# A graph attention layer over sorted edges: 64 instead of 16 groups of edges computed without gathering, in four rounds

## The chip, the cores and the metric

The kernel runs on one core of one Trainium2 chip. The metric is the device time of one execution in microseconds, as the median of several runs.

## The reference

One layer of a graph network with attention, a residual sum and a layer norm. N = 12,500 nodes with 64 features, E = 400,000 edges with 64 features. Edges come sorted by destination; destinations are drawn as 12500 times the square of a uniform number, so the first nodes have by far the most edges.

```python
h_src, h_dst = x[src], x[dst]
e = leaky_relu(concat([h_src, h_dst, edge]) @ W_attn + b_attn, 0.01)[:, 0]
m = concat([h_src, edge]) @ W_ne
alpha = segment_softmax(e, dst)                    # over the edges of one destination
z = segment_sum(alpha[:, None] * m, dst)
out = layernorm(x + relu(concat([x, z]) @ W_out))  # eps 1e-5, no scale
```

## The kernel before

**Groups and batches.** A group is 512 edges (`GE`), 128 partitions by 4 (`T`); there are 782 groups. 16 of them (`BS`) make a batch; the last three batches hold 12, 12 and 6 (`ENDS`). A batch is cut into tiles of four groups (`SG`). The first `DG` groups, "dense" groups, are in no batch; here `DG` is 16, which leaves 766 groups in 49 batches.

**Gathers.** For every group of a batch, POOL issues four indirect DMAs (`gather`, L271). Each fetches 128 rows of sources into a `zx` tile; a row is a score part (one number) and x (64 numbers), from `table` in DRAM, which the front writes. In batch 0 the rows come from x itself. There are eight `zx` tiles, two batches' worth. Nothing else runs on POOL during the loop.

**A batch.** `scores` (per tile, as its rows arrive) forms the raw scores of its edges and a one-hot matrix `hot` of the edges' destinations among a window of `S` nodes. `softmax` (once a batch, behind the last tile's scores) runs scans over the 2048 edges and yields `alpha`. It calls `fill()` at four pauses. `weights` multiplies `hot` by `alpha`, `products` sums rows of `zx` by matmul into a PSUM bank `pg`, and `add_in` adds the bank into `acc`, a ring of sums by node. The products of the first two tiles (`NOW`) follow the batch's own softmax; those of the other two go on the list `later` and are done in the pauses of the next batch's softmax (`some_products`). A tile's buffer is free for POOL when its products are done.

**Finished nodes.** When all edges of a block of four times 128 nodes are in `acc`, `finish0` to `finish3` compute the output of these nodes, in pieces spread over the batches. `due` says behind which batch a block may go.

**Dense groups.** The first 16 groups belong to a handful of nodes each, so their rows need not be gathered. Three steps replace it, spread over the batches two groups at a time (`EACH`):

- Picks (batches 1 to 8). `look_turn` and `look_products` form on ACT and PE a one-hot matrix of the sources' low seven bits times the score parts of all nodes; `look_scores` picks on DVE by the high bits and adds the edge part and the destination part.
- A dense softmax behind batch 8 (`softmax` with `d`), its weights put into `kept`.
- Counts (batches 9 to 16). `dense_counts` and `dense_sum` build, for all 12,500 sources, the sum of weights by destination (`counts`); `dense_weights` and `products` with k = None add the edge features into `acc`. `resolve` multiplies `counts` by x (L418), picks the diagonal blocks on DVE (L421, L424) and adds the result into `acc`.

**Order.** The order on PE, DVE, ACT and SP in the loop is the order in which the program is written (`manual_schedule`): each engine runs its instructions in that order and waits for whatever the next one needs. POOL runs ahead through the gathers as lists of sources arrive and zx tiles come free. In the last two tiles of a batch (slots 0 and 1 of `EACH`), and in the softmax pauses (`meanwhile`), the dense work is placed:

```python
slot = i - (len(lots[k]) - EACH)
...
def meanwhile():
    while seen:
        look_scores(*seen.pop(0))
    if open_counts:
        dense_sum(*open_counts.pop(0))
    add_up(1)
    some_products()
```

**The front.** Before the loop, the score parts of all nodes are computed, `table` is written, destination windows are gathered, and the dense groups' lists are loaded and split (`dense_list`, `dense_places`), while POOL gathers batch 0 from x.

**A fallback.** The kernel looks at the data's spread while it runs (`fars`, `ups`, `lates`, `earlies`, `raised`) and runs a general path behind this one if a bound does not hold.

Of the kernel before, what the change touches and what calls it, by code (L numbers as in the profile page):

```python
# [9 lines left out]
F32 = mybir.dt.float32  # L10
# [5 lines left out]
P = 128  # L16
T = 4
# [17 lines left out]
DB = 1  # L35
EACH = 2
NOD = 5
# [10 lines left out]
def sorted_path(ctx, tc, x, dst, idx, edge, w_ne, w_attn, b_attn, w_out, out, flag):  # L48
# [43 lines left out]
    SD_ = width(DG)  # L92
    NK = len(sizes)

    def node_at(e, sigmas):
        e = e + sigmas * (e * (1.0 - e / E)) ** 0.5
        return int(N * (max(e, 0.0) / E) ** 2)

    bases = [node_at(g * GE, -5.0) for g in range(DG)]
    assert all(node_at((g + 1) * GE, 5.0) < b + NOD for g, b in enumerate(bases))  # L100
    ND = max(bases[d * BS + BS - 1] + NOD - bases[d * BS] for d in range(DB))
    HC = min(8, P // ND)

# [3 lines left out]
    mrows = [const.tile([1, 2, P + 2], F32, name=f"tops{i}") for i in range(2)]  # L107
    srows = [const.tile([1, 2, P + 2], F32, name=f"dens{i}") for i in range(2)]
    for i in range(2):
        nc.vector.memset(d3s[i], N)  # L110
        nc.vector.memset(mrows[i], FLOOR)
        nc.vector.memset(srows[i], 0.0)
# [19 lines left out]
    fars = const.tile([P, NK + 2 * DB], F32, name="fars")  # L132
    ups = const.tile([P, NK + DB], F32, name="ups")
    earlies = const.tile([P, NK + DB + 1], F32, name="earlies")
# [11 lines left out]
    low, high, place, kept, slot_, y_dense = (  # L146
        const.tile([P, T, DG], F32, name=n) for n in ("low", "high", "place", "kept", "slot_", "y_dense"))
    d3d = [const.tile([P, P + 2], I32, name=f"dense_edges{d}") for d in range(DB)]
    for d in range(DB):
        nc.vector.memset(d3d[d], N)  # L150
    counts = const.tile([P, NB, ND], F32, name="counts")
    own = const.tile([HC * ND, HC], F32, name="own")
    nc.vector.tensor_reduce(own, ident[0:HC * ND, 0:HC * ND].rearrange("p (h n) -> p h n", n=ND), axis=AX.X, op=OP.add)
    node = const.tile([HC * ND, ND], F32, name="node")
    nc.vector.tensor_reduce(node, ident[0:HC * ND, 0:HC * ND].rearrange("p (h n) -> p n h", n=ND), axis=AX.X, op=OP.add)
    meet = const.tile([1, 2], I32, name="meet")
    of_next = const.tile([1, 4], F32, name="of_next")
    held = const.tile([1, 2], F32, name="held")
# [24 lines left out]
    soft = psum.tile([P, 512], F32, name="soft", bufs=1)  # L183
    yraw, ev, scan1, scan2 = cut(soft, T * BG, P, P, P)
# [11 lines left out]
    def dense_list(d):  # L196

        srcs = pre.tile([P, BS, 2 * T], I32, name="dense_srcs", bufs=1)
        nc.sync.dma_start(out=srcs, in_=idx[d * BS:(d + 1) * BS].rearrange("g p c -> p g c"))
        return srcs  # L200

    def dense_places(d, srcs):
# [10 lines left out]
        for c, by in ((NK + d, d0b[:, at]), (NK + DB + d, base_row[:, at])):  # L213
            to = slot_ if c == NK + d else place
            nc.vector.tensor_tensor(to[:, :, at], pp, by.unsqueeze(1).to_broadcast([P, T, BS]), op=OP.subtract)
            nc.vector.tensor_reduce(fars[:, c:c + 1], to[:, :, at], axis=AX.XY, op=OP.max)
            nc.vector.tensor_scalar(fars[:, c:c + 1], fars[:, c:c + 1], 1.0 - (SD_ if c == NK + d else NOD), None, op0=OP.add)
        nc.vector.tensor_reduce(earlies[:, NK + d:NK + d + 1], place[:, :, at], axis=AX.XY, op=OP.min)
        nc.vector.scalar_tensor_tensor(place[:, :, at], high[:, :, at], -float(NOD), place[:, :, at], op0=OP.mult, op1=OP.subtract)

# [142 lines left out]
    def look_scores(g, j, loads, found):  # L363
# [16 lines left out]
        nc.vector.tensor_reduce(y_dense[:, :, g], total.rearrange("p c t -> p t c"), axis=AX.X, op=OP.add)  # L380

    def dense_counts(g):
# [3 lines left out]
        for t in range(T):  # L386
# [3 lines left out]
            nc.vector.tensor_scalar(lows[:, t, :], count_, low[:, t, g:g + 1], kept[:, t, g:g + 1],  # L390
# [7 lines left out]
    def dense_sum(g, to):  # L398

        b = bases[g] - bases[g // BS * BS]  # L400
        at = counts[:, :, b:b + NOD]
        nc.vector.tensor_tensor(at, at, to.rearrange("p (h n) -> p h n", n=NOD), op=OP.add)

    def dense_weights(g0, n):

        w = work.tile([P, SG, T, S], F32, name="w", bufs=4)[:, :, :, 0:SD_]
        for j in range(n):
            nc.vector.tensor_tensor(w[:, j], slots[:, 0:SD_].unsqueeze(1).to_broadcast([P, T, SD_]),
                                    slot_[:, :, g0 + j:g0 + j + 1].to_broadcast([P, T, SD_]), op=OP.is_equal)
            nc.vector.tensor_tensor(w[:, j], w[:, j], kept[:, :, g0 + j:g0 + j + 1].to_broadcast([P, T, SD_]), op=OP.mult)  # L410
        return w

    def resolve(d):
# [6 lines left out]
        mine = big().rearrange("l p t -> l (p t)")[0:HC * ND, 0:HC * D].rearrange("p (h f) -> p h f", f=D)  # L420
        nc.vector.tensor_tensor(mine, pairs[0:HC * ND, 0:HC * D].rearrange("p (h f) -> p h f", f=D),  # L421
                                own.unsqueeze(2).to_broadcast([HC * ND, HC, D]), op=OP.mult)
        sums_ = work.tile([P, D], F32, name="sums_", bufs=1)
        nc.vector.tensor_reduce(sums_[0:HC * ND, :], mine.rearrange("p h f -> p f h"), axis=AX.X, op=OP.add)  # L424
        if d + 1 < DB:
            nc.vector.memset(counts, 0.0)
        z = psum.tile([P, SG, P], F32, name="pg", bufs=4)[0:D, 0, 0:ND]
        nc.tensor.matmul(z, sums_[0:HC * ND, :], node, start=True, stop=True)
        at = acc[0:D, bases[d * BS]:bases[d * BS] + ND]
        nc.vector.tensor_tensor(at, at, z, op=OP.add)  # L430
# [10 lines left out]
    def turned(table_):  # L441
        line = tiny.tile([1, 2, P], F32, name="line")
# [1086 lines left out]
```

## Time and profile before

| | |
|---|---|
| median of 3 runs | 3908.24 us (3907.86 to 3909.37) |
| profiled execution, its own time | 3900.66 us |
| span of the profiled execution | 3898.9 us |
| busy: POOL | 2900.7 us (74%), 3080 instructions |
| busy: DVE | 1753.5 us (45%), 4329 instructions |
| busy: PE matmul, weight load | 1685.3 us (43%), 1541.1 us (40%) |
| busy: ACT | 729.7 us (19%) |
| mean granted TensorE clock | 0.617 |

The span runs from the first to the last instruction on the core. Busy shares are of the span. PE's matmuls and weight loads overlap. A group in the profile is one source line with one kind of instruction: its count, its busy time and mean duration, then the idle time of the engine just in front of it and what ended that idle time ("issue": nothing the profile shows).

### The profile page before, as it was taken

What the parts mean: (1) busy time and instruction counts of PE and PEld (TensorE: products, weight loads), DVE (VectorE), ACT (ScalarE), POOL (GpSimd) and SP (SyncE); (2) the same over time, 40 slices, a digit from 0 to 9 for tenths busy, and PEclk for the clock granted to TensorE, in tenths of its full rate; (3) what the DMA queues carried; (4) which work ended last, traced back from release to release, by engine and by line L of the source; (5) the groups of instructions that cost most, each with busy time, mean ns of one, the idle gap of its engine ahead of it and who ended that gap; (6) DMA issues with size and microseconds to landing.
All of it is one profiled execution on the core that took longest, in us unless ns stands there. A gap on an engine that the chain in (4) does not pass through costs nothing.

```text
span 3898.9 us, 30077 instructions
## 1 busy us (share of the span) xinstructions
PE 1685.3 (43%) x7735; PEld 1541.1 (40%) x7735; DVE 1753.5 (45%) x4329; ACT 729.7 (19%) x1711; POOL 2900.7 (74%) x3080
## 2 busy tenths in 40 slices
PE   0254334354555445533444334533354334543364
PEld 0244334343344334433344324432344334433363
DVE  5443334443444434443444434544444444544465
ACT  1111111132222211121111111111111111111121
POOL 6777777777777777777777777777777777777773
PEclk9999999975555555555555555555555555555555
DMA  9323223232333223232323223322323223223221
GB/s 119 71 62 68 56 57 71 55 66 54 62 61 66 55 51 64 54 65 54 64 54 65 54 53 66 64 50 60 61 60 67 55 54 67 61 53 63 53 59 30
DMA packets 456065, 236.40 MB, mean 61 GB/s; under 512 B 298371, under 2 KB 406906, under 8 KB 455882
## 3 DMA queue, kind: packets, MB, share of 16 engines
q0 software_dynamic: 98272, 102.21, 16.7%
q1 hardware_dynamic: 354566, 131.85, 14.1%
q8 instruction: 63, 1.03, 0.1%
q14 instruction: 120, 0.98, 0.1%
q10 hardware_dynamic: 3044, 0.33, 0.1%
HBM read 227.47 MB, written 6.68 MB: 60 GB/s over the span
## 4 chain that ended last, share of the span: by engine, by line
POOL 43%; issue 18%; PE 18%; DVE 10%; DMA 9%; ACT 1%; DVEq 1%; SPq 0%; POOLq 0%; ACTq 0%
POOL zx L271 43%; PE pg L634 13%; DMA zx<-table,srcs 7%; DVE acc L651 1%; DMA zx<-in_x_dram,srcs 1%; PE pg L841 1%; PE lines L436 1%; DVE hot L314 1%; DVE pr L319 1%; DVE sdst L322 1%; PE lines L439 1%; PE pg L840 1%; DVE level L575 1%; PE pg L395 1%; DVE soft L531 0%
## 5 line engine op out<-in xcount | busy, mean ns | idle before, releaser
L271 POOL DMA_INDIRECT zx<-table,srcs x3000 | 2830.3, 943 | 914.3 <-issue 869.5
L634 PEld LDWEIGHTS pg<-w,zx 128*128 128x128 f32 x5984 | 1286.0, 329 | 62.7 <-issue 31.6
L634 PE MATMUL pg<-w,zx 128*128 128x12 f32 (+10 forms) x5984 | 1292.5, 387 | 41.9 <-issue 24.6
L436 PE MATMUL lines<-ident,bnd 128*1 128x128 f32 x200 | 57.4, 388 | 1676.4 <-ACT bnd L534 1663.5
L436 PEld LDWEIGHTS lines<-ident,bnd 128*1 128x1 f32 x200 | 12.8, 95 | 1689.4 <-ACT bnd L534 1670.9
L312 DVE TENSOR_TENSOR fixed<-fixed,zx 128x16 f32<-128x16 f32 (+2 forms) x196 | 36.2, 184 | 1353.7 <-DMA zx<-table,srcs 1351.3
L305 DVE TENSOR_TENSOR pr<-ze,fixed 128x1024 f32<-128x1024 f32 (+2 forms) x196 | 234.3, 1195 | 113.9 <-ACT fixed L302 113.6
L302 ACT ACTIVATE fixed<-wrow 128x144 f32<-128x144 f32 (+9 forms) x196 | 50.2, 256 | 1022.2 <-DVE soft L323 444.7
L307 DVE TENSOR_REDUCE fixed<-pr 128x16 f32<-128x1024 f32 (+2 forms) x196 | 235.9, 1203 | 6.7
L395 PE MATMUL pg<-big,lows 128*128 128x490 f32 x128 | 90.9, 878 | 279.0 <-DVE lows L390 271.7
L303 ACT ACTIVATE zx<-ze 128x1024 f32<-128x1024 f32 (+2 forms) x196 | 203.8, 1040 | 10.6 <-DMA zx<-table,srcs 1.3
L651 DVE TENSOR_TENSOR acc<-acc,pg 128x12 f32 (+11 forms) x782 | 141.7, 181 | 93.9 <-DVE acc L651 27.6
L529 ACT ACTIVATE soft<-turned 128x128 f32<-128x128 f32 x50 | 19.5, 389 | 865.0 <-DVE turned L527 850.9
L395 PEld LDWEIGHTS pg<-big,lows 128*128 128x128 f32 x128 | 36.8, 303 | 327.3 <-issue 163.0
L617 DVE TENSOR_TENSOR w<-hot,fixed 128x576 f32<-128x576 bf16 (+9 forms) x196 | 103.2, 585 | 51.3 <-PE pg L634 51.3
L314 DVE TENSOR_TENSOR hot<-fixed,drel 128x576 bf16<-128x576 f32 (+9 forms) x196 | 116.9, 597 | 7.5 <-DVE fixed L312 0.8
L319 DVE TENSOR_TENSOR pr<-hot,fixed 128x576 f32<-128x576 bf16 (+9 forms) x196 | 116.1, 592 | 6.7
L322 DVE TENSOR_REDUCE sdst<-pr 128x16 f32<-128x192 f32 (+11 forms) x196 | 116.0, 592 | 6.8
L572 DVE SCALAR_TENSOR_TENSOR soft<-mask,lines,soft 128x128 f32<-128x128 f32 x50 | 18.0, 360 | 143.4 <-PE lines L439 143.4
L271 POOL DMA_INDIRECT zx<-in_x_dram,srcs x64 | 61.8, 966 | 27.2 <-issue 17.7
L481 ACT ACTIVATE same<-step 128x129 f32<-128x129 f32 x50 | 15.6, 312 | 332.4 <-DVE ups L479 332.4
L841 PE MATMUL pg<-both,acc 128*128 128x64 f32 x184 | 63.2, 447 | 19.5 <-DVE acc L651 16.3
(234 smaller groups left out, 1667.9 us busy)
## 6 DMA issues: line engine op xcount, KB each, us to landing
ze<-in_edge_dram SPq DMA_DIRECT2D x184, 512.0 KB
zx<-table,srcs POOLq DMA_INDIRECT x3000
table<-xall SPq DMA_DIRECT2D x7, 455.0 KB
out_dram<-yo SPq DMA_DIRECT2D x24, 128.0 KB
ze<-in_edge_dram SPq DMA_DIRECT2D x8, 384.0 KB
edges_of<-in_dst_dram SPq DMA_DIRECT2D x184, 8.1 KB
xall<-in_x_dram SPq DMA_DIRECT2D x13, 224.0 KB
srcs<-in_idx_dram SPq DMA_DIRECT2D x45, 64.0 KB
```

Source lines behind the costliest of these rows:

```text
L271: nc.gpsimd.indirect_dma_start(out=zx[0:r, g, t, 1:EW] if plain else zx[0:r, g, t, 0:EW], out_offset=None, in_=x[:, :] if plain else table ...
L303: nc.scalar.activation(zx[0:r, 0:n, :, EW:EW + D], ze[0:r, 0:n], AF.Copy)
L305: nc.vector.tensor_tensor(pr[0:r, 0:n], ze[0:r, 0:n], w_edge[0:r].unsqueeze(1).to_broadcast([r, n, T, D]), op=OP.mult)
L307: nc.vector.tensor_reduce(ysum[0:r, 0:n], pr[0:r, 0:n], axis=AX.X, op=OP.add)
L314: nc.vector.tensor_tensor(hot[0:r, 0:n], slots[0:r, 0:Sk].unsqueeze(1).unsqueeze(1).to_broadcast([r, n, T, Sk]), drel[0:r, :, b:b + n].rea ...
L319: nc.vector.tensor_tensor(at[0:r, 0:n], hot[0:r, 0:n], win[0:r, 0:n, 0:Sk].unsqueeze(2).to_broadcast([r, n, T, Sk]), op=OP.mult)
L322: nc.vector.tensor_reduce(sdst[0:r, 0:n], at[0:r, 0:n], axis=AX.X, op=OP.add)
L395: nc.tensor.matmul(to, lows[:, t, :], highs[t], start=(t == 0), stop=(t == T - 1))
L436: nc.tensor.transpose(in_order(line), col, ident)
L617: nc.vector.tensor_tensor(w[0:r, 0:n], hot[0:r, 0:n], alpha[0:r, :, b:b + n].rearrange("p t g -> p g t").unsqueeze(3).to_broadcast([r, n, ...
L634: nc.tensor.matmul(pg[:, g, :], zx[:, g, t, 1:EW + D], w[:, g, t, :], start=(t == 0), stop=(t == T - 1))
L651: nc.vector.tensor_tensor(ag, ag, pg[r0:P, g, :], op=OP.add)
```

## The change

`DB` goes from 1 to 4: four rounds of 16 dense groups, 64 in all, so 718 groups remain in 46 batches (three batches of 16 fewer). Each round has its picks, its dense softmax and its counts; the counts of one round run in the same batches as the picks of the next. Picks of round d fall in batches 8d + 1 to 8d + 8, the dense softmaxes behind batches 8, 16, 24 and 32, counts in 9 to 40.

- Dense sums have an array of their own, `accd`, indexed by the true node number, which is read from memory at run time (`node_of`); before, the sums with x went to places in `acc` fixed at compile time. It is added to `acc` when blocks 1 to 3 are finished; node block 0 is finished apart, after the last dense sum.
- Products with x are done after every fourth dense group (`CH`), for windows of 16 nodes (`ND`): `node_products` on PE behind the first tile's scores, `node_pick` on DVE ahead of the third tile's, `node_sum` behind the fourth's. `counts` is cleared for each.
- Edge features' sums get a place of their own in PSUM (`z_edge`), where they took a bank `pg`: `edge_products` behind the first tile's scores, `edge_sum` ahead of the third's. `dense_weights` uses a tile `wd` of its own.
- Picks and counts are issued one tile earlier (`slot = i - 1`) and taken up on DVE ahead of the next tile's scores, not in the softmax's pauses.
- Behind a batch with a dense softmax all four tiles go on `later`, and the dense softmax's pauses run `some_products`.
- Some buffers are halved (`tops`, `dens`, `line`, `rw`, `sq`), and `high` and `slot_` are bf16.

The core of the diff:

```diff
-DB = 1
+DB = 4
 EACH = 2
+CH = 4
+ND = 16
+HC = 8
...
-    SD_ = width(DG)
+    SD_ = NOD
...
+    z_edge = fixed[D:P, 512 - EACH * NOD:512].rearrange("p (g n) -> p g n", n=NOD)
+    z_node = fixed[0:D, 512 - EACH * NOD - ND:512 - EACH * NOD]
...
     def dense_sum(g, to):
-        b = bases[g] - bases[g // BS * BS]
-        at = counts[:, :, b:b + NOD]
+        _, vs = nc.values_load_multi_w_load_instructions(
+            rel[0:1, g:g + 1], engines=(EngineType.DVE,), min_val=0, max_val=ND - NOD,
+            skip_runtime_bounds_check_because=within)
+        at = counts[:, :, ds(vs[0], NOD)]
         nc.vector.tensor_tensor(at, at, to.rearrange("p (h n) -> p h n", n=NOD), op=OP.add)
...
-        w = work.tile([P, SG, T, S], F32, name="w", bufs=4)[:, :, :, 0:SD_]
+        w = tiny.tile([P, EACH, T, SD_], F32, name="wd", bufs=1)
...
+    def edge_products(g0, n, ep, w):
+        for g in range(n):
+            for t in range(T):
+                nc.tensor.matmul(z_edge[:, g, :], ep[:, g, t, :], w[:, g, t, :], start=(t == 0), stop=(t == T - 1))
+    def edge_sum(g0, n):
+        for g in range(n):
+            at = accd[D:P, ds(node_of(g0 + g), NOD)]
+            nc.vector.tensor_tensor(at, at, z_edge[:, g, :], op=OP.add)
...
+    def node_pick(g0, pairs):
+        mine = big().rearrange("l p t -> l (p t)").rearrange("p (h f) -> p h f", f=D)
+        nc.vector.tensor_tensor(mine, pairs.rearrange("p (h f) -> p h f", f=D),
+                                own.unsqueeze(2).to_broadcast([P, HC, D]), op=OP.mult)
+        sums_ = work.tile([P, D], F32, name="sums_", bufs=1)
+        nc.vector.tensor_reduce(sums_, mine.rearrange("p h f -> p f h"), axis=AX.X, op=OP.add)
+        if g0 + CH < DG:
             nc.vector.memset(counts, 0.0)
+        nc.tensor.matmul(z_node, sums_, node, start=True, stop=True)
...
         def meanwhile():
-            while seen:
-                look_scores(*seen.pop(0))
-            if open_counts:
-                dense_sum(*open_counts.pop(0))
             add_up(1)
             some_products()
...
-                    slot = i - (len(lots[k]) - EACH)
+                    slot = i - 1
...
+                    if i == 2 and edges_of:
+                        edge_sum(*edges_of[0:2])
+                    if i == 2 and opened:
+                        opened = node_pick(*opened)
+                    while seen:
+                        look_scores(*seen.pop(0))
+                    while open_counts:
+                        dense_sum(*open_counts.pop(0))
                     hot = scores(g0, n, tiles[i], drel, b0, k == 0)
+                    if i == 0:
+                        if chunk_of is not None:
+                            opened = node_products(chunk_of)
+                        if edges_of:
+                            edge_products(*edges_of)
+                    if i == 3 and opened is not None:
+                        node_sum(opened)
...
-                    ws = [weights(g0, n, hot, b0) for g0, n, zx, hot in parts]
+                    for i, (g0, n, zx, hot) in enumerate(parts):
+                        later.append([k, g0, n, zx, weights(g0, n, hot, b0), b0, fac if i == 0 else None, 0, None])
...
-                    fac_d, dense_carry = softmax(k + 1, lines_of(*after), dense_carry, lambda: None, d)
+                    fac_d, dense_carry = softmax(k + 1, lines_of(*after), dense_carry, some_products, d)
```

More of the change, by code (lines that the diff above doesn't have):

```diff
@@ L196, in dense_list @@
     def dense_list(d):
-        srcs = pre.tile([P, BS, 2 * T], I32, name="dense_srcs", bufs=1)
+        srcs = pre.tile([P, BS, 2 * T], I32, name="dense_srcs", bufs=DB)
         nc.sync.dma_start(out=srcs, in_=idx[d * BS:(d + 1) * BS].rearrange("g p c -> p g c"))
@@ L212, in dense_places @@
         nc.scalar.activation(pp, srcs[:, :, T:2 * T].rearrange("p g t -> p t g"), AF.Copy)
[L213 to L219, printed above, removed]
+        to, c = slot_[:, :, at], slice(NK + d, NK + d + 1)
+        nc.vector.tensor_tensor(to, pp, d0b[:, at].unsqueeze(1).to_broadcast([P, T, BS]), op=OP.subtract)
+        nc.vector.tensor_reduce(fars[:, c], to, axis=AX.XY, op=OP.max)
+        nc.vector.tensor_scalar(fars[:, c], fars[:, c], 1.0 - NOD, None, op0=OP.add)
+        nc.vector.scalar_tensor_tensor(place[:, :, at], high[:, :, at], -float(NOD), to, op0=OP.mult, op1=OP.subtract)
     def listed(k):
@@ L389, in dense_counts @@
             nc.scalar.activation(hi, hi, AF.Relu, scale=-1.0, bias=1.0)
-            nc.vector.tensor_scalar(lows[:, t, :], count_, low[:, t, g:g + 1], kept[:, t, g:g + 1],
+            nc.vector.tensor_scalar(lows[:, t, :], count_, low[:, t, g:g + 1], kept[:, t, g % BS:g % BS + 1],
                                     op0=OP.is_equal, op1=OP.mult)
@@ L825, in behind_front @@
     def behind_front(c0, po):
-        a0 = c0 * P % RING
         unwrap(c0)
-        for j in range(min(NBC, NB - c0)):
-            nc.tensor.matmul(po[:, j, :], acc[:, a0 + j * P:a0 + (j + 1) * P], both, start=False, stop=True,
+        for j in range(size_of(c0)):
+            nc.tensor.matmul(po[:, j, :], sums_of(c0, j), both, start=False, stop=True,
                              skip_group_check=True)
@@ L834, in finish2 @@
     def finish2(c0, xtt):
-        n = min(NBC, NB - c0)
-        a0 = c0 * P % RING
+        n = size_of(c0)
         unwrap(c0)
```

239 lines of the change are left out of this document (128 added, 111 removed).

## The prediction

> **What bounds the kernel now.** I read the page first: the span, the groups, the chain of work that ended last. One group stands out on every count.
>
> ```profile
> span 3898.9 us, 30077 instructions
> POOL 6777777777777777777777777777777777777773
> POOL 43%; issue 18%; PE 18%; DVE 10%; DMA 9%; ACT 1%; DVEq 1%; SPq 0%; POOLq 0%; ACTq 0%
> L271 POOL DMA_INDIRECT zx<-table,srcs x3000 | 2830.3, 943 | 914.3 <-issue 869.5
> L271 POOL DMA_INDIRECT zx<-in_x_dram,srcs x64 | 61.8, 966 | 27.2 <-issue 17.7
> ```
>
> POOL is level from the second slice to the last, and the idle time in front of its gathers is "issue": a fixed pause between two instructions, not a wait for anybody. The chain gives POOL only 43%, because it steps to other engines where work happened to end together; the list of POOL's waits settles whether POOL ever stood.
>
> ```profile
> POOL zx L271 <- issue: 887.2, 2911, 0.3
> POOL zx L271 <- DMA zx<-table,srcs: 20.4, 67, 0.3
> POOL zx L271 <- PE pg L634: 12.2, 40, 0.3
> POOL zx L271 <- DMA zx<-in_x_dram,srcs: 6.5, 4, 3.5
> ```
>
> No entry on the table gathers has a longest wait over 0.3 us, which is the issue pause itself with another name. So POOL never waits for a released zx tile. Only the front has real waits (6.5 us in all). POOL's timeline gives the pitch and the tail:
>
> ```profile
> 100.62 0.94 POOL L271 DMA_INDIRECT zx<-table,srcs  x1 [0.30 <-issue]
> 3844.08 0.86 POOL L271 DMA_INDIRECT zx<-table,srcs  x1 [0.30 <-issue]
> ```
>
> 3000 gathers start within 3844.08 - 100.62 = 3743.46 us: 3743.46 / 2999 = 1.2482 us each, 79.89 us for the 64 of a batch of 16 groups. Behind the last one lie 3898.9 - 3844.9 = 54 us of tail. Windows of one batch each, set on that pitch, show whether any stage departs from it:
>
> ```profile
> core 0: us, PE busy (x) PEld busy (x) DVE busy (x) ACT busy (x) POOL busy (x), PEclk, DMA share, GB/s
> 433.10:513.00 79.90, 33.82 (x157) 32.50 (x157) 33.41 (x94) 13.15 (x32) 60.39 (x65) 1.00 0.31 63
> 752.60:832.50 79.90, 42.34 (x172) 33.48 (x173) 40.72 (x117) 26.06 (x65) 60.39 (x65) 0.91 0.29 59
> 992.30:1072.20 79.90, 41.79 (x179) 34.49 (x178) 33.90 (x94) 20.59 (x44) 60.40 (x65) 0.57 0.30 61
> 1471.60:1551.40 79.80, 43.07 (x180) 33.21 (x178) 32.85 (x81) 10.57 (x28) 60.29 (x65) 0.59 0.29 57
> 1631.30:1711.20 79.90, 35.21 (x161) 33.28 (x160) 33.61 (x83) 14.77 (x35) 60.39 (x65) 0.50 0.30 59
> 3708.20:3788.10 79.90, 54.87 (x246) 51.10 (x245) 48.99 (x125) 17.88 (x45) 60.40 (x64) 0.50 0.29 58
> ```
>
> In this order: a batch with dense picks, the one behind the dense softmax, one with dense counts, the one with the dense products with x, a plain one, a crowded one near the end. POOL takes 60.4 us of busy time in each. The kernel is a string of gathers; the other engines are about half empty.
>
> **Part 1: gathers taken away.** 16 dense groups become 64. Four gathers a group: 48 x 4 = 192 gathers fewer (2808 + 64 remain of 3000 + 64), exactly three batches. 192 x 1.2482 = 239.7 us off POOL's string, if POOL stays unblocked. With them go three batches of scores, softmax and products, which were hidden.
>
> **Part 2: dense work for 48 more groups.** It rides in the batches, two groups at a time: picks in batches 1 to 32, dense softmaxes behind batches 8, 16, 24, 32, counts in 9 to 40, products with x after every fourth group. So batches 9 to 32 now carry picks and counts together. The costs:
>
> ```profile
> L371 DVE TENSOR_TENSOR hits<-pps,high 128x392 bf16<-128x392 f32 x16 | 8.9, 555 | 0.0
> L374 DVE TENSOR_REDUCE total<-pg 128x4 f32<-128x392 f32 x16 | 9.1, 566 | 0.5
> L369 DVE TENSOR_REDUCE total<-pr 128x4 f32<-128x256 f32 x16 | 6.7, 420 | 0.6
> L379 DVE TENSOR_REDUCE total<-pr 128x4 f32<-128x16 f32 x16 | 2.7, 170 | 0.5
> L402 DVE TENSOR_TENSOR counts<-counts,pg 128x490 f32<-128x490 f32 x16 | 10.6, 660 | 23.6 <-PE pg L395 23.6
> L390 DVE TENSOR_SCALAR lows<-pps,low,kept 128x128 f32<-128x128 f32 x64 | 21.7, 401 | 0.0
> L884 DVE MEMSET counts<- 128x882 f32 x1 | 0.8, 793 | 0.1
> L360 PE MATMUL pg<-s_src,big 128*128 128x98 f32 x128 | 34.6, 449 | 72.7 <-ACT big L353 72.7
> L395 PE MATMUL pg<-big,lows 128*128 128x490 f32 x128 | 90.9, 878 | 279.0 <-DVE lows L390 271.7
> 1482.50 13.22 PE L418 MATMUL pg<-xall,counts 128*72 128x512 f32 x26
> 1495.76 0.69 DVE L421 TENSOR_TENSOR big<-pg,own 72x512 f32<-72x512 f32 x1 [12.25 <-PE pg L418]
> 1496.48 1.02 DVE L424 TENSOR_REDUCE sums__7505<-big 72x64 f32<-72x512 f32 x1
> 1479.10 0.36 DVE L651 TENSOR_TENSOR acc<-acc,pg 64x4 f32 x2 [0.62 <-issue]
> ```
>
> DVE, a batch: two picks of three wide steps at 0.56, two at 0.42 and four small ones at 0.17 = 3.2 each, 6.4; two counts of 21.7/16 + 0.66 = 2.0 each, 4.0; edge sums 0.4 and four small steps for weights, 1 together; every second batch a pick of nodes, 0.69 + 1.02, and a clearing of counts, 0.79 x 1568/882 = 1.41, with its sums 3.3. Together under 15 us on the 33.6 of a plain batch: 49, which is what DVE does in the crowded window. PE: 35.2 plain + 34.6/8 = 4.3 to twice that for picks (they ran at clock 1.00, counts at 0.57) + 90.9/8 = 11.4 for counts + 13.2 for products with x + about 1 for edges = 65 to 70 of 79.9. Both stay below POOL's 79.9, so I put this work at nothing: its cover is the time in which DVE and PE wait for gathers.
>
> **What could still block POOL** is a zx tile freed late; there are eight, so batch k + 2 takes those of batch k. Tightest is the third tile of a batch, whose products are put off into the next batch's softmax:
>
> ```profile
> 914.50 3.43 PE L634 MATMUL pg<-w,zx 128*128 128x16 f32 x16
> 939.55 0.95 POOL L271 DMA_INDIRECT zx<-table,srcs  x1 [0.30 <-issue]
> ```
>
> Its last product ends at 917.9, POOL reaches the tile at 939.5: a softmax may come 21 us late before POOL stands. The batch behind a dense softmax is the place:
>
> ```profile
> 821.15 0.19 DVE L312 TENSOR_TENSOR fixed<-fixed,zx 128x16 f32<-128x16 f32 x1 [13.29 <-DMA zx<-table,srcs]
> ```
>
> There DVE had caught up and still waited 13.3 us for the fourth tile. The change puts in front of that row two picks (6.4), the second count (2.0, behind it before), edge sums (0.4) and the pick of nodes (3.3): 12.1, so 1.2 us to spare. If DVE must also wait for the whole of the products with x (13.2), it is 12 us late, still under 21. The products with x lie in PE ahead of the picks' and counts' matmuls, so those queue behind them, but PE has nothing nearer the end in that stretch. The dense softmax now has the batch's own products in its pauses instead of behind it, which frees the first tiles earlier. SP's additions (256 KB of edges again, two 128 KB rows a batch) sit in front of the next edge load; the DMA share of 0.29 to 0.31 leaves room. Bounds for Part 2: 0 to about 10 us in each of three such batches, 30 us; a gain is excluded, since POOL has no wait there to lose. I take 0, by the waits row without a single stall.
>
> **Part 3: the front.** Three more lists of 64 KB in 32-byte pieces, rows of low parts for 64 groups, and four times the list arithmetic. The nearest rows are the one list of before and POOL's wait ahead of it:
>
> ```profile
> 69.77 0.39 SPq L199 DMA_DIRECT2D dense_srcs<-in_idx_dram  x1
> 76.14 0.22 DVE L207 TENSOR_SCALAR parted<-dense_srcs 128x64 int32<-128x64 int32 x1 [25.23 <-DMA dense_srcs<-in_idx_dram]
> 63.80 0.94 POOL L271 DMA_INDIRECT zx<-in_x_dram,srcs  x1 [3.52 <-DMA zx<-in_x_dram,srcs]
> ```
>
> A list took 6 us to land, so batch 0's scores may start up to 3 x 6 = 18 us later, plus 5 of DVE. Nothing hangs on that: the first reuse of a zx tile is 64 gathers after 100.62, at 180.5, and the first batch's weights were ready at
>
> ```profile
> 127.75 0.88 DVE L617 TENSOR_TENSOR w<-hot,fixed 128x128 f32<-128x128 bf16 x4
> ```
>
> with some 50 us over. But the traffic may hold POOL's own first gathers as at 63.80. Bounds: -6.5 (the front's waits go, if the traffic falls elsewhere) to +12 (two thirds of the three lists); I take +2, near the row of 3.5.
>
> **Part 4: the tail.** The same last three batches; the new first block is finished ahead of them, and the open block's finish stays where it was. 0, bounds -3 and +3, since only the order of a few ACT instructions differs.
>
> **Sum.** The profiled execution took 3900.7 us by its own time (1.8 more than its span), the median of the three runs is 3908.24, 7.6 above. 3900.7 - 239.7 + 2 = 3663.0 profiled; with the same 7.6 us, **3670.5**. (What a measurement of this kernel can tell from no change is some 0.2%, 8 us.)
>
> **Rivals.**
>
> *POOL stands in the dense batches.* Late softmaxes behind the dense softmax or the products with x, since DVE waits in order for PE there. Against: 21 us of room and the arithmetic above. For: both waits meet in batches 17, 25 and 33, and DVE's scores grow with the windows, which eats the 13.3. At 10 us for each of three or four: 3680 to 3710. Chance 0.13.
>
> *The added DVE work slows the gathers themselves.* DVE busy goes from 33.4 to 49.0 us between the second and the last window and POOL's 64 or 65 instructions take 60.4 in both; the counts' L390 ran in the window from 992 and cost POOL nothing. If POOL were shut out for as long as the added counts and clearings run, 48 x 21.7/16 + 15 x 1.41 = 86 us: 3757. Chance 0.02. The Trainium skill (SBUF — State Buffer, "Who interferes with whom") says that some VectorE forms take a port pair shared with GpSimd for a whole instruction and starve descriptor generation, and counts tensor_scalar among them; that speaks against this change. The windows do not show it for the forms used here.
>
> *PE becomes the bound: slower than before.* If PE's in-order queue, with picks, counts, products with x and a batch's own products, took more than 79.9 us, POOL would follow PE. The gain is gone when the 32 batches with counts take 239.7/32 = 7.5 us more each, 87.4 us; at 90 us it is 32 x 10.1 = 323 us, 3992. For: the counts matmuls average 878 ns at a low clock, so my 65 to 70 rests on overlap. Against: the crowded window holds 54.9 of matmul and 51.1 of weight loads at clock 0.50 and POOL does not stretch. Chance 0.03.
>
> *It doesn't do what it says.* A dense group may span five nodes at most, or the kernel falls back on its general path. Destinations are 12500 x u^2 sorted; at edge 32768 that is node 84, and 512 edges span 2.6 nodes. No chance given.
>
> **Chances.** Forecast (3661 to 3682: the front and tail bounds) 0.82, POOL standing 0.13, ports 0.02, PE 0.03. The low end is 3670.5 less 6.5 + 2 + 1 at the front and tail, 3661; the high end takes in most of the first rival, 3700. Faster 0.96, same 0.01, slower 0.03.
>
> **What would show it.** Right: one POOL pitch of 1.248 us from start to end, no POOL wait on table gathers above 0.3 us, windows of 79.9 us with POOL at 60.4 in batches 9 to 40, DVE near 45 and PE near 65 there, a tail of 54 us. Wrong: POOL waits for PE or DMA of several us at the batches behind a dense softmax (first rival), a mean gather above 943 ns (second), windows in which PE has no idle time and POOL's share falls (third), or an added wait before 100 us (front).

## The result: 4.4% faster, and POOL stood still for 66 us

| | before | after |
|---|---|---|
| median (lowest to highest) | 3908.39 us (3907.86 to 3909.37) | 3735.15 us (3733.94 to 3736.5) |
| ratio | | 0.9557, interval 0.954 to 0.9573 |
| profiled execution, its own time | 3900.66 us | 3736.5 us |
| its span | 3898.9 us | 3734.8 us |
| mean granted clock | 0.617 | 0.68 |

The forecast was 3670.5 us (3661 to 3700). The direction was right; 65 us of the gain are missing. The page and the waits of the kernel after, beside the rows of before in the prediction (POOL's gathers are now on L273, the scores' sum with the gathered part on L314):

```profile
span 3734.8 us, 34021 instructions
POOL 6777777777777777777777766777775777777773
POOL zx L273 <- issue: 884.0, 2684, 28.6
DVE pr L307 <- ACT fixed L304: 505.6, 60, 22.4
ACT fixed L304 <- PE fixed L427: 444.1, 28, 23.9
L273 POOL DMA_INDIRECT zx<-table,srcs x2808 | 2654.2, 945 | 921.8 <-issue 866.9
```

POOL's row of tenths now has three dips behind the middle, and its longest wait is 28.6 us where it was 0.3. "issue" hides the reason: POOL's gather waits for a free zx tile, which the profile does not name. The timeline of POOL gives the first and last gather from the table and, between them, every stand of over 0.9 us (last column: the idle time ahead of the row):

```profile
102.64 0.94 POOL L273 DMA_INDIRECT zx<-table,srcs  x1 [0.30 <-issue]
1986.49 0.94 POOL L273 DMA_INDIRECT zx<-table,srcs  x1 [3.85 <-issue]
2164.22 0.95 POOL L273 DMA_INDIRECT zx<-table,srcs  x1 [18.04 <-issue]
2331.94 0.94 POOL L273 DMA_INDIRECT zx<-table,srcs  x1 [7.95 <-issue]
2495.97 0.95 POOL L273 DMA_INDIRECT zx<-table,srcs  x1 [4.30 <-issue]
2660.00 0.95 POOL L273 DMA_INDIRECT zx<-table,srcs  x1 [4.33 <-issue]
2740.63 0.95 POOL L273 DMA_INDIRECT zx<-table,srcs  x1 [0.95 <-issue]
2848.90 0.95 POOL L273 DMA_INDIRECT zx<-table,srcs  x1 [28.55 <-issue]
3677.52 0.87 POOL L273 DMA_INDIRECT zx<-table,srcs  x1 [0.30 <-issue]
```

The seven stands sum to 67.97 us, 65.9 more than seven usual pauses of 0.3. All lie behind 1980 us, the two large ones behind the dense softmaxes of batches 24 (at 2077) and 32 (at 2757). The difference of the spans closes with that:

| term | predicted | measured, from |
|---|---|---|
| 192 gathers at 1.2482 | -239.7 | -239.7 (2808 gathers from the table, were 3000) |
| front | +2 | +2.0 (first gather at 102.64, was 100.62) |
| stands of POOL | 0 | +65.9 |
| pitch elsewhere | 0 | +5.3 (3677.52 - 102.64 = 3574.9, less 2807 x 1.2482 = 3503.7 and the stands; a gather took 945 ns, was 943) |
| tail | 0 | +2.4 (3734.8 - 3678.4 = 56.4, was 54.0) |
| sum | -237.7 | -164.1 = 3734.8 - 3898.9 |

**Where the time is lost.** Windows of two pitches (159.8 us). The first fence is the kernel before, where neither picks nor counts run at that time; the second is the kernel after, where both do (columns: window, its length, busy time and instructions of PE, PEld, DVE, ACT and POOL, then clock, DMA share, GB/s):

```profile
1641.40:1801.20 159.80, 70.43 (x318) 66.58 (x318) 67.30 (x168) 29.55 (x68) 120.79 (x129) 0.50 0.30 59
```

```profile
1641.40:1801.20 159.80, 110.07 (x418) 86.97 (x419) 88.35 (x226) 48.83 (x99) 120.83 (x128) 0.57 0.32 67
```

No engine is full: PE has 50 us of idle time in two batches, DVE 71. Yet the batches fall behind in that stretch. The transpose that opens a softmax (DVE L555) stands in the timeline of the kernel after, for batches 8, 16, 17 and 23, at

```profile
746.04 0.32 DVE L555 STREAM_TRANSPOSE turned<-soft 128x128 f32<-128x128 f32 x1
1387.93 0.32 DVE L555 STREAM_TRANSPOSE turned<-soft 128x128 f32<-128x128 f32 x1
1481.60 0.31 DVE L555 STREAM_TRANSPOSE turned<-soft 128x128 f32<-128x128 f32 x1
1975.75 0.30 DVE L555 STREAM_TRANSPOSE turned<-soft 128x128 f32<-128x128 f32 x1
```

From batch 8 to 23, 15 pitches of 79.89 us would be 1198.4; it took 1229.7. Batch 23 is 31 us late against POOL, and there the stands begin. By the same sum batch 16 is 2.8 us late and batch 17, the one behind the second dense softmax, 16.5. So 14 us came in one step, which was not won back, and the other 15 over the six batches from 17 to 23. The timeline of PE, ACT and DVE between 1667 and 1687 us shows what a batch waits for:

```profile
1667.24 0.27 ACT L304 ACTIVATE fixed<-wrow 128x112 f32<-128x112 f32 x1 [4.95 <-DVE w L642]
1669.56 13.69 PE L656 MATMUL pg<-w,zx 128*128 128x24 f32 x64
1683.18 1.87 PE L427 MATMUL fixed<-wd,ep 128*64 128x5 f32 x16
1685.09 0.27 ACT L304 ACTIVATE fixed<-wrow 128x112 f32<-128x112 f32 x1 [14.19 <-PE fixed L427]
1685.38 1.22 DVE L307 TENSOR_TENSOR pr<-ze,fixed 128x1024 f32<-128x1024 f32 x1 [12.73 <-ACT fixed L304]
```

L304 copies a tile's destination windows into the PSUM bank `fixed`; L307 multiplies by them and is the first step of the tile's scores. The change put the edge sums, `z_edge`, into ten columns of the same bank. PE writes them (L427) behind the batch's own products (L656, 13.7 us) and in every second batch behind the products with x too. ACT's copy for the second tile goes to other columns of that bank, but waits until L427 is done; DVE waits for ACT, and everything of the batch waits behind DVE. That is 28 waits of ACT with 444 us in all, up to 23.9 each. DVE's own wait for ACT's copy is 505.6 us in the kernel after; in the kernel before it was

```profile
DVE pr L305 <- ACT fixed L302: 113.6, 142, 6.6
```

**Theories.** A: this wait in the shared bank makes each batch with counts a little longer than POOL's pitch, the lead runs out (the time by which a tile comes free before POOL reaches it), and POOL stands. B: the dense softmaxes, some 22 us of DVE, ACT and PE in a row, push the batches, and the wait in the bank is covered.

### The profile page after: what moved, and what is told of

It is laid out like the page before. It is cut to its first block, busy times and chain, and to the rows that moved or that the text cites. A ratio compares the mean times of both kernels' runs of the same rounds, so it can differ in the third digit from the quotient of the medians.

```text
span 3734.8 us, 34021 instructions
## 1 busy us (share of the span) xinstructions
PE 2224.6 (60%) x8923; PEld 1801.7 (48%) x8923; DVE 2013.0 (54%) x5075; ACT 1018.3 (27%) x2205; POOL 2723.6 (73%) x2888
## 5 line engine op out<-in xcount | busy, mean ns | idle before, releaser
L273 POOL DMA_INDIRECT zx<-table,srcs x2808 | 2654.2, 945 | 921.8 <-issue 866.9
L656 PE MATMUL pg<-w,zx 128*128 128x24 f32 (+10 forms) x5600 | 1222.1, 391 | 44.2 <-issue 41.7
L656 PEld LDWEIGHTS pg<-w,zx 128*128 128x128 f32 x5600 | 1217.7, 332 | 63.5 <-issue 50.2
L397 PE MATMUL pg<-big,lows 128*128 128x490 f32 x512 | 370.8, 894 | 505.5 <-DVE lows L392 425.9
L307 DVE TENSOR_TENSOR pr<-ze,fixed 128x1024 f32<-128x1024 f32 (+3 forms) x184 | 219.2, 1191 | 505.9 <-ACT fixed L304 505.6
L304 ACT ACTIVATE fixed<-wrow 128x144 f32<-128x144 f32 (+10 forms) x184 | 48.7, 264 | 1103.6 <-PE fixed L427 444.1
L309 DVE TENSOR_REDUCE fixed<-pr 128x16 f32<-128x1024 f32 (+3 forms) x184 | 221.1, 1202 | 6.3
L440 PE MATMUL pg<-xall,counts 128*128 128x512 f32 (+1 forms) x416 | 209.8, 665 | 10.6 <-DVE earlies L1049 10.6
L305 ACT ACTIVATE zx<-ze 128x1024 f32<-128x1024 f32 (+3 forms) x184 | 191.7, 1042 | 10.5 <-issue 1.3
L314 DVE TENSOR_TENSOR fixed<-fixed,zx 128x16 f32<-128x16 f32 (+3 forms) x184 | 33.9, 184 | 287.7 <-DMA zx<-table,srcs 282.5
L390 ACT ACTIVATE big<-places,place 128x490 f32<-128x490 f32 x256 | 176.0, 687 | 0.0
L673 DVE TENSOR_TENSOR acc<-acc,pg 128x16 f32 (+10 forms) x718 | 132.2, 184 | 80.2 <-DVE acc L673 38.2
L391 ACT ACTIVATE big<-big 128x490 f32<-128x490 f32 x256 | 156.7, 612 | 8.2
L557 ACT ACTIVATE soft<-turned 128x128 f32<-128x128 f32 x50 | 19.4, 388 | 445.7 <-DVE turned L555 445.7
```

What stands on the lines that cost most here:

```text
L273: nc.gpsimd.indirect_dma_start(out=zx[0:r, g, t, 1:EW] if plain else zx[0:r, g, t, 0:EW], out_offset=None, in_=x[:, :] if plain else table ...
L305: nc.scalar.activation(zx[0:r, 0:n, :, EW:EW + D], ze[0:r, 0:n], AF.Copy)
L307: nc.vector.tensor_tensor(pr[0:r, 0:n], ze[0:r, 0:n], w_edge[0:r].unsqueeze(1).to_broadcast([r, n, T, D]), op=OP.mult)
L309: nc.vector.tensor_reduce(ysum[0:r, 0:n], pr[0:r, 0:n], axis=AX.X, op=OP.add)
L390: nc.scalar.activation(hi, places, AF.Square, bias=place[:, t, g:g + 1])
L391: nc.scalar.activation(hi, hi, AF.Relu, scale=-1.0, bias=1.0)
```

## The experiments

Except where a second kind of chip is named, the runs below fell on two chips on which the kernel before took 3901.8 and 3902.0 us. "Late" always means by the sum above: against batch 8 and a pitch of 79.89 us.

**The changed kernel again**, as the control of the runs below.

> The changed kernel itself, beside the kernel before, on the chip that the next three run on. If this chip gives its usual times, both theories expect 3735 us beside 3908 (ratio 0.956) and POOL standing still for 71 us between its gathers. If it gives 4588 us for the kernel before, as in the four runs before these, both theories expect the changed kernel above 5200 us, and the next three are then compared with this run and not with 3735.

3731.93 us, ratio 0.9564 (0.9545 to 0.9583); the stands sum to 68.2 us over the usual pauses. This is the kind of chip of the prediction, and the times below compare with 3732, or with 3731 on the second of the two chips.

**Edge products at the end of the batch before.**

```diff
                     if i == 0:
                         if chunk_of is not None:
                             opened = node_products(chunk_of)
-                        if edges_of:
-                            edge_products(*edges_of)
...
                     edges_of = (batch_counts[0], len(batch_counts), rows_again,
                                 dense_weights(batch_counts[0], len(batch_counts)))
+                    edge_products(*edges_of)
```

> The edge products are issued at the end of the batch before, ahead of that batch's own products, instead of behind the next batch's. Theory A (ScalarE's copy of the second tile's windows waits in the bank `fixed` for the edge products, which lie behind 13.7 us of the batch's own products and in every second batch behind 13.2 us of products with x): no edge product is late, the copy of the windows waits under 3 us, POOL stands under 10 us in all, 3665 us (3660 to 3675). Theory B (the 22 us of each dense softmax push the batches behind POOL, and the wait in the bank is hidden): 3735 us.

3663.69 us (3662.99 to 3664.67), ratio 0.939 (0.9375 to 0.9406). The waits:

```profile
POOL zx L273 <- issue: 818.1, 2685, 0.3
DVE fixed L314 <- DMA zx<-table,srcs: 488.3, 73, 13.9
DVE pr L307 <- ACT fixed L304: 55.0, 60, 6.6
```

POOL never stands, and the same softmaxes come at

```profile
742.36 0.32 DVE L555 STREAM_TRANSPOSE turned<-soft 128x128 f32<-128x128 f32 x1
1942.16 0.30 DVE L555 STREAM_TRANSPOSE turned<-soft 128x128 f32<-128x128 f32 x1
```

1199.8 us apart: 1.4 late in place of 31. The dense softmax behind batch 16 still makes batch 17 late, by 8.0 us, but batch 18 is only 1.2 late. DVE waits for gathers again (488 us, the kernel after 282). This is what theory A forecast. The new place is not free: in front of the edge products PE now waits 75 us in all for their weights, and DVE's own weights wait 53 us for the edge products. POOL's string shows nothing of either.

**Edge products where they were, in a bank of their own.**

```diff
     def edge_products(g0, n, ep, w):
+        z_edge = psum.tile([P, SG, P], F32, name="pg", bufs=4)[D:P, 0, 0:EACH * NOD].rearrange("p (g n) -> p g n", n=NOD)
+        edge_at.append(z_edge)
...
     def edge_sum(g0, n):
+        z_edge = edge_at.pop()
```

> The edge products stay where they are in TensorE's queue, but write a bank of the ring `pg`, taken when they are issued and free when they are added, in place of the bank `fixed`. Theory A: the copy of the windows no longer waits for them, VectorE's sums of the edges wait instead, two tiles later, when they are long done; the ring of four banks is one bank shorter for a third of a batch, which may cost up to 1 us in a batch: 3665 to 3690 us. Theory B: 3735 us. Were it the edge products' length in TensorE's queue and not the bank, it would stay at 3735 too.

3662.12 us (3661.76 to 3665.46), ratio 0.9388 (0.9372 to 0.9404):

```profile
POOL zx L273 <- issue: 815.6, 2676, 0.3
DVE pr L307 <- ACT fixed L304: 55.4, 60, 7.0
100.54 0.94 POOL L273 DMA_INDIRECT zx<-table,srcs  x1 [0.30 <-issue]
3604.24 0.87 POOL L273 DMA_INDIRECT zx<-table,srcs  x1 [0.31 <-issue]
```

The matmuls, their order and their length in PE's queue are those of the changed kernel (the edge products take 47.5 us in both); only the bank differs, and all 68 us of stands are gone. So it is the bank, not PE's time. 3604.24 - 100.54 = 3503.7 us is the unbroken string of 2808 gathers to a tenth. One bank fewer for the products in part of a batch cost nothing that can be seen. This and the one above are the fastest kernels here that do all the work, within 2 us of each other.

**The order of two calls.** In place of moving the edge products out of the batch, they go ahead of the products with x only.

```diff
                     if i == 0:
+                        if edges_of:
+                            edge_products(*edges_of)
                         if chunk_of is not None:
                             opened = node_products(chunk_of)
-                        if edges_of:
-                            edge_products(*edges_of)
```

> Only the order of two calls is swapped: the edge products go into TensorE's queue ahead of the products with x (13.2 us in every second batch), and still behind the batch's own products (13.7 us). On the first kind of chip: if both lengths of queue count alike, a pair of batches becomes 13 us shorter, 151 to 153 us against the 159.8 us of its gathers, no batch falls behind, 3663 to 3670 us. If the wait behind the batch's own products is enough by itself to make the batches fall behind, part of the stands stays: 3680 to 3715 us.

3678.72 us (3677.59 to 3683.08), ratio 0.9427 (0.9411 to 0.9442). It fell between the two ranges expected. The products with x were the larger part: of the 67 us between the changed kernel (3730.85 on the same chip) and the one with the edge products moved, 52 went with this swap. The profiled execution, the slowest of the four, still has ACT wait 309.8 us for L427, 14.7 at most, and POOL stands 1.7, 1.1 and 9.7 us. The batch's own products alone do not make one batch after the other later: batch 16 is 1.7 us late, batch 17 behind the dense softmax 15.8, batch 23 12.7. What they do is keep the batches from winning the push of a softmax back.

**Without dense softmaxes**, the wait in the bank kept. The dense groups' weights are then whatever the last scores left.

```diff
-                    fac_d, dense_carry = softmax(k + 1, lines_of(*after), dense_carry, some_products, d)
+                    lines_of(*after)
+                    fac_d = None
+                    for _ in range(4):
+                        some_products()
```

> The four dense softmaxes are left out (their weights are whatever the last scores give); every product that they covered is still issued. Theory A: the batches still fall behind by 2 to 3 us each through the bank, only the push of 22 us at the end of each round is gone: 3685 to 3715 us. Theory B: 3665 us, with no stand of POOL.

3700.28 us, one run. POOL's stands in its timeline:

```profile
2306.27 0.94 POOL L273 DMA_INDIRECT zx<-table,srcs  x1 [7.87 <-issue]
2470.39 0.94 POOL L273 DMA_INDIRECT zx<-table,srcs  x1 [4.64 <-issue]
2634.38 0.94 POOL L273 DMA_INDIRECT zx<-table,srcs  x1 [4.53 <-issue]
2812.28 0.94 POOL L273 DMA_INDIRECT zx<-table,srcs  x1 [18.37 <-issue]
3293.13 0.94 POOL L273 DMA_INDIRECT zx<-table,srcs  x1 [1.48 <-issue]
```

35 us of stands are left without any dense softmax. The first three have the size of those at 2332, 2496 and 2660 us in the kernel after; its stands of 3.9 and 18.0 are gone, and 28.6 has become 18.4. Batch 16 is 0.6 us late here, batch 23 19.4: the wait in the bank alone makes batches late, from batch 16 on. Theory B falls as the cause; but 32 us did go with the softmaxes. Are they a cost by themselves?

**Both: edge products moved, and no dense softmaxes** (the two diffs together).

> The edge products issued at the end of the batch before, and the four dense softmaxes left out as well. On the first kind of chip, if the softmaxes are hidden wherever the batches have a lead, nothing is left to win: 3661 to 3666 us; if they cost something beside their push on late batches: under 3660 us.

3661.62 us, one run, against 3663.7 with the softmaxes. With the wait the four softmaxes cost 3731.9 - 3700.3 = 32 us, without it 2, which is within the spread of runs of one kernel. They only bring out what the wait has done to the lead: a batch that is on time takes a push of 22 us and wins it back, one that is already late does not.

**Three rounds in place of four** (`DB = 3`), the wait in the bank kept.

> Three rounds of dense groups in place of four, and the wait in the bank as it was. Unbroken, POOL's string would be 79.9 us longer than in the repaired kernels: 3743 us. The picks and the counts then run together over 16 batches in place of 24. On the first kind of chip, by the theory of a lead that the batches use up: POOL stands 0 to 25 us in all, 3743 to 3768 us. If every round cost its 18 us of stands by itself: about 3793 us.

3758.05 us (3755.26 to 3758.35), ratio 0.9629 (0.9613 to 0.9645), with one stand:

```profile
2151.19 0.94 POOL L273 DMA_INDIRECT zx<-table,srcs  x1 [13.11 <-issue]
```

The time is in the range expected of a lead that is used up, and far from 18 us a round: 12.8 us of stands over 16 batches with picks and counts together, 68 over 24. A steady loss it does not show: batch 18 is 9.6 us late, batch 24 12.2, and the one stand comes with batch 25, behind a dense softmax, 36.2 us late. So the fourth round took 79.9 us of gathers away, and as the change was written 27 us of it arrived.

**A second kind of chip.** Eight runs, on two other chips, show something else altogether. The kernel before takes 4588 us there (4588.28 on one, 4587.89 on the other). The first four of these runs were to decide between A and B. Expected of the edge products at the end of the batch before, of the two calls swapped, of the dense softmaxes left out, and of the edge work left out (`edge_products` and `edge_sum`, so that the dense nodes' sums lack their edge half):

> Edit: the products of the dense edge features (into z_edge, in the PSUM bank of tile fixed) go to PE at the end of the batch before, ahead of that batch's own products, not behind the first tile's scores. Theory A (shared bank): ACT's copy of the second tile's windows into fixed waits for these products, which lie in PE behind 13.7 us of the batch's products and, in every second batch, 13.2 us of products with x; DVE idles for it, batches come later and later, and POOL stands 70 us in the end. Then the wait of ACT for the edge products goes, POOL stands under 5 us, time 3665 (3660 to 3675). Theory B (the dense softmax): its 22 us push the batch behind past what the eight zx tiles can bear, whatever stands in the bank; then POOL stands about as long as now, 3735 (3720 to 3740).

> Edit: the two calls behind the first tile's scores are swapped, edge products ahead of products with x. Theory A: the second tile's copy still waits behind the batch's own products in every batch, but no longer for the 13.2 us of products with x in every second one; a pair of batches falls from 165 us to about 152 to 158, just under POOL's 159.8, so POOL stands 0 to 15 us: 3665 to 3680. Theory B: nothing changes, 3735. If DVE's wait for the products with x at its own pick of nodes is what counts, 3735 too, since that pick comes no earlier.

> Leaves out the four dense softmaxes (the batch's own weights are taken as the dense ones); all else as in the changed kernel. Theory A: batches still fall behind by 5 to 6 us a pair while picks and counts run together (12 pairs, 60 to 70 us against 21 us of room), so POOL still stands, 20 to 50 us: 3685 to 3715. Theory B: POOL stands under 5 us, 3665.

> Leaves out the products and sums of the dense edge features altogether. Theory A: the copy of the second tile's windows has nothing to wait for, POOL does not stand, 3660 to 3668. Theory B: 3730 to 3735 (only the 1.9 us of products and 0.4 us of sums a batch go).

Four more fell on the other of these chips: the two calls swapped, three rounds, edge products moved with no dense softmaxes, and no edge work again:

> Only the order of two calls is swapped: the edge products go into TensorE's queue ahead of the products with x (13.2 us in every second batch), and still behind the batch's own products (13.7 us). If both lengths of queue count alike, a pair of batches becomes 13 us shorter, 151 to 153 us against the 159.8 us of its gathers: no batch falls behind, POOL never stands, 3663 to 3670 us. If the wait behind the batch's own products is enough by itself to make the batches fall behind, part of the 71 us stays: 3680 to 3715 us.

> The changed kernel with three rounds of dense groups in place of four (48 groups not gathered, 64 gathers more), and the wait in the bank as it was. Unbroken, POOL's string would be 79.9 us longer than in the repaired kernels: about 3743 us. The picks and the counts then run together over 16 batches (8 to 24) in place of 24, and in the changed kernel the lead that the batches have over POOL lasted just until batch 24: by the theory of the bank POOL stands 0 to 25 us in all, 3743 to 3768 us. So the fourth round, as it stands, bought little more than 10 to 35 us of the 80 us of its gathers. If the lead did not matter and every round cost its 18 us, the stands would be about 50 us and the time 3793 us.

> The edge products issued at the end of the batch before, and the four dense softmaxes left out as well. With the softmaxes left out and the wait kept POOL stood 37 us (3700 us); with the wait taken away and the softmaxes kept it never stood (3664 us). If the softmaxes cost something by themselves beside their push on late batches, it shows here: under 3660 us. If they are hidden wherever the batches have a lead, nothing is left to win: 3661 to 3666 us.

> The edge products and the sums that they go into are left out altogether (128 x 4 small matmuls and 64 sums less; the dense nodes' edge half is then missing from the output). What is left besides is the dense weights. If the move of the edge products to another bank or another place already hides all of their cost, this gains nothing over it: 3661 to 3667 us. Below 3655 us they would still cost in the repaired kernels.

All eight missed by over 1300 us:

| kernel | time there | instructions | ns of span per instruction |
|---|---|---|---|
| before | 4588 us | 30077 | 153 |
| edge products at the end of the batch | 5185.23, ratio 1.1303 (1.1284 to 1.1322) | 34068 | 152 |
| order of two calls | 5254.87, ratio 1.1446 (1.1423 to 1.1469); again 5257.47 | 34021 | 154 |
| no dense softmaxes | 5299.75 | 33774 | 157 |
| no edge products and sums | 5016.79; again 5024.67 | 32786 | 153 |
| three rounds | 5105.42, ratio 1.1131 (1.1112 to 1.1149) | 32813 | 155 |
| edge products moved and no softmaxes | 5122.96 | 33821 | 151 |

(Spans are those of the profiled executions; for the kernel before the median stands in.)

Neither theory could be tested there: this kind of chip says nothing of A and B, and as the kernel with no edge work ran on this kind alone, its forecast stays open. The page of the kernel with two calls swapped, there:

```profile
span 5255.9 us, 34021 instructions
L273 POOL DMA_INDIRECT zx<-table,srcs x2808 | 2648.9, 943 | 2446.8 <-issue 2309.0
L656 PE MATMUL pg<-w,zx 128*128 128x24 f32 (+10 forms) x5600 | 1231.9, 376 | 974.0 <-issue 907.5
```

and the same rows of the changed kernel, the control above:

```profile
L273 POOL DMA_INDIRECT zx<-table,srcs x2808 | 2650.2, 944 | 923.7 <-issue 870.4
L656 PE MATMUL pg<-w,zx 128*128 128x24 f32 (+10 forms) x5600 | 1222.1, 391 | 44.3 <-issue 41.9
```

One gather and one matmul take no longer than on the first kind. What grows is the idle time ahead of single instructions for which the profile shows no wait: PE has 907.5 us of it ahead of its plain products. On POOL it comes in lumps. Between 290 and 810 us POOL stands 6.3 to 6.8 us ahead of every 32nd gather and the usual 0.3 ahead of all others, as in

```profile
298.66 0.94 POOL L273 DMA_INDIRECT zx<-table,srcs  x1 [6.33 <-issue]
344.64 0.94 POOL L273 DMA_INDIRECT zx<-table,srcs  x1 [6.35 <-issue]
```

The traces of two more kernels there (edge products at the end of the batch, no edge work) have the same lumps in that stretch; on the first kind there is none. Over these programs time there goes along with the number of instructions, not with POOL's string; whatever adds dense work adds instructions, and every variant of the change is 9 to 16% slower than before. The changed kernel itself ran on chips of the first kind alone; its last run was expected so:

> The changed kernel itself, to show which chip the next three run on. On the first kind (kernel before 3902 us) it takes 3732 us, and the next three are read against that and against the 3664 us of the kernel with the edge products at the end of the batch. On the second kind (kernel before 4588 us) all kernels so far took 151 to 157 ns for each instruction of their profile, so that this one, with 34021 instructions, should take 5150 to 5340 us whatever the wait in the bank does.

It took 3730.85 us. So on the second kind of chip the changed kernel is not measured.

## Why the prediction was wrong

- **Part 1 was right.** 192 gathers at 1.2482 us are off the string; with the wait taken away the string is 3503.7 us as worked out, and 0.939 of the prediction's median, 3908.24, is 3669.8 us against the forecast of 3670.5. The rest of the dense work does cost nothing then, as forecast.
- **Part 2 is the step that failed**: "I put this work at nothing". Its sums of busy time were not short: two batches hold 110 of PE and 88 of DVE, 55 and 44 each, where 65 to 70 and 49 were reckoned. What failed is the sentence that the products with x delay only picks and counts, "but PE has nothing nearer the end in that stretch". It had: the edge products lie behind them, and through the bank `fixed` they hold ACT's copy and the second tile's scores. The term was taken at 0, with bounds of 0 to 30, and measured 65.9.
- The change listed `z_edge = fixed[...]`, and the prediction priced the edge matmuls (1 us) and their sums (0.4), but never asked who else uses that bank. The rule was to be had: the Trainium skill (PSUM — Partial Sum Buffer, "PSUM bank collisions raise a hardware error") says that engines must be kept apart by bank and group of partitions, not by address. Here the two writers share 64 partitions of one bank and no column, and the traces show them kept apart, at 444 us of ACT's waits; a bank of its own ends it. What keeps them apart the traces do not say, and whether the columns could be written at the same time was not tried.
- **"1.2 us to spare", "21 us late before POOL stands".** The room was the right quantity and nearly of the right size (the first stand, 3.6 us, came with batch 23 31 us late, so some 28 us of room), but it was spent in one place, the batch behind a dense softmax. It is a stock: the 14 us of one softmax were still missing when the next 15 came. Without the wait the same softmax costs 8.0 us at batch 17 and 1.2 at batch 18. A lead must be checked against the sum over a stage, and not in its worst batch alone.
- **The first rival** (POOL stands) is what happened: behind the dense softmaxes of batches 24 and 32, as it named, not behind that of 16, and at other batches. It had DVE wait for PE, but by arithmetic and not through a bank. Its price, 10 us in three or four places, was about half of the true one.
- **Ports**: refuted at 86 us. The count tensor_scalar steps went from 64 to 256 and DVE from 45 to 54%, while a gather took 943 ns before, 945 after, and 943 to 946 in the runs above, with no order in DVE's load. These steps read a PSUM tile; other forms were not run. **PE as the bound**: not seen; PE is idle for 50 of 159.8 us in that stretch.
- **Front and tail**: +2.0 and +2.4 against +2 and 0. The match of the front is luck: in two later profiles of the changed kernel the first gather stands at 100.1 and 99.9 us. The 5.3 us of pitch too belong to this one execution: a gather took 944 and 943 ns in the later two.
- **Slips in the working** that change nothing: DVE's 33.4 us are those of the first window of the list, the second holds 40.7; the low end of the range takes 1 us for the tail where Part 4 bounds it at 3; the third rival's sum gives 3994, not 3992.

## What to carry to other kernels

When a change gives data a place in a buffer that other steps use, list every step that writes or reads that bank, and look where each stands in its engine's queue: an access to other columns can wait for all that lies ahead of the last writer. Busy time of 55 of 80 us is no proof of cover when an engine works in order; ask for the chain of one batch, and whether it is longer than the pitch. Lateness adds up unseen: here POOL first stood at batch 23, six batches behind the first large step, so the first stand lies far from its cause.

## What was not expected of the hardware

The chips differ: the same kernel before took 3902 to 3908 us on some and 4588 on others, with gathers of equal length (943 and 944 ns). On the second kind time followed the number of instructions, 151 to 157 ns each over seven programs. That engines there are short of instructions is read from the idle time called "issue" and not shown. The lumps ahead of every 32nd gather speak for something that comes in blocks, but no run tells fetching instructions apart from issuing them. The Trainium skill (Runtime: NRT & Kernel Launch, "Instruction fetch mechanics") calls the cost of crossing from one fetched block to the next mostly hidden. No run here can say whether it is on those chips.
